# A residual added on TensorE: layer 0 of a two-layer model, the sum copied out by ScalarE

## The chip, the core and the metric

The kernel runs on one core of a Trainium2 chip. Five engines work side by side, each with its own queue of instructions in a fixed order: TensorE (PE in the profile, its weight loads as PEld), VectorE (DVE), ScalarE (ACT), GpSimd (POOL) and SyncE (SP), which here only starts transfers. TensorE reads SBUF and writes its sums to PSUM, in banks of 128 partitions x 512 float32; DVE and ACT can read and write PSUM and SBUF. The metric is the device time of one execution in microseconds, as the median of the runs shown; a profiled execution of its own gives the trace.

## What is computed

A batch of 2 sequences of 1024 rows, 512 wide, goes through two layers. Cut to what matters here:

```python
x = L0_attn_x                                   # (2, 1024, 512)
xn = layernorm(x)
x = x + L0_attn(xn) + L0_ffn(xn)                # layer 0
xn = layernorm(x)
x = x + L1_attn(xn) + L1_ffn(xn)                # layer 1

def L0_attn(x):                                 # one head of 128
    qkv = x @ Wqkv + bqkv
    q, k, v = split(qkv)
    out = softmax(q @ k.T / sqrt(128)) @ v
    return out @ Wo + bo                        # (1024, 128) @ (128, 512)

def L0_ffn(x):                                  # four streams of 128
    H_res = sinkhorn(logits(x), 50 rounds)      # 4 x 4 for each row
    ...
    return mix(H_res, x) + branch(x)
```

The change touches the first sum of layer 0: `x + (out @ Wo + bo)`.

## The kernel before

**Tiles.** A sequence is a batch `b` (0 or 1) of eight tiles `t` of 128 rows. `acc[b, t]` (128 x 512 float32, in SBUF for the whole kernel) is loaded with x (`load_x`, L124 to L127) and collects every term that is added to the residual stream. Matmuls take float16 operands: a float32 value is split into a high and a low half, and a product of two such values is three passes (`PASSES`, L81: high x high, high x low, low x high), all into one PSUM bank.

**Layer 0.** `front0(b)` makes the layer norm, transposes it into `xT` (through SP's DMA transposes, L242), and forms the logits of the Sinkhorn step (L385) and Q, K and V. `sinkhorn(b)` then runs 49 rounds; for batch 0 `chain_dve` does them on DVE, six small instructions a round (L576 to L578 and L581 to L583), each needing the one before, and at the end L592 and L527 write `Hm`, the 4 x 4 mixing matrix of each row. `attn0_rows` makes the score rows of four tiles at a time (L287 on DVE takes the row minimum out of PSUM, L291 on ACT the exponential, L305 to L314 the split on ACT, POOL and DVE, L320 the transposes on SP); `attn0_out` multiplies them with V and projects. `branch0` and `branch0_add` (POOL, L451 and L455) add the branch's output to `acc`. `mix0_units` mixes the streams by `Hm`: some tiles on ACT and POOL (L633, L634), some on DVE (L642), these after a copy of `acc` to PSUM by ACT (L614).

**`attn0_out`, which the change edits** (L467 to L488). Once for each half of a batch, four times in all. L476 and L478 on ACT and L479 on POOL turn the attention's output into two float16 halves `hl`. Then for each of four tiles a bank `p` is taken (`PP`, three banks in rotation, `BP` = 3). L484 puts the bias row `bo` into it, as two matmuls of one partition; L486 adds the three passes of the projection with `Wo`. All operands carry factors whose product is 1024. L488 on DVE scales the bank by 1/1024, adds `acc[b, t]` and writes the sum back to `acc[b, t]`.

**What sets the order.** The program is written as one long sequence of Python calls; a planner then orders the instructions of each engine by their place in the program and by a timeline that it simulates, and the queues are fixed before the run. So an instruction can stand in its queue ahead of its place in the text when the planner found it ready early: the bias rows L484 run long before the projection that they belong to. Steps of the Sinkhorn chain of batch 0 are drawn between the rows of attention by calls of `adv`. Buffers with one tag rotate through a fixed number of slots; the tag `tw` has one slot, which `ffn_block` of layer 1 uses from L954 on. POOL writes masks and constants at the very start (L111 to L120), then issues the loads of `Wlat` (L656).

**Layer 1.** `start` projects latents, Q, K and V from `xT` of batch 0's new layer norm, and `layer1_attn` runs eight groups of heads over both batches, with the rest of batch 1's layer 0 work (its Sinkhorn chain on POOL, its mix) and the feed-forward blocks laid between the rows.

Of the kernel before, what the change touches and what calls it, by code (L numbers as in the profile page):

```python
# [11 lines left out]
AF = mybir.ActivationFunctionType  # L12
ALU = mybir.AluOpType
# [3 lines left out]
P = 128  # L17
# [34 lines left out]
def tile_model(ctx: ExitStack, tc: tile.TileContext, out: bass.AP, a: dict):  # L52


    nc = tc.nc
    V, A, G = nc.vector, nc.scalar, nc.gpsimd
# [7 lines left out]
    def T(tag, shape, dt=F32, bufs=None):  # L64
        count[0] += 1
        kw = {} if bufs is None else {"bufs": bufs}
        return sb.tile(shape, dt, tag=tag, name=f"{tag}_{count[0]}", **kw)

    def C(name, shape, dt=F32):
        return const.tile(shape, dt, tag=name, name=name)  # L70

    def PP(shape=(P, 512)):
        count[0] += 1
        return ps.tile(list(shape), F32, tag="pp", name=f"pp_{count[0]}", bufs=BP)
# [40 lines left out]
        G.affine_select(mh, mh, [[-1, QR]], ALU.is_ge, NEG, base=0, channel_multiplier=1)  # L115
    ones = C("ones", [P, P], F16)
    G.memset(ones, 1.0)
    pm = C("pm", [P, 8])
    for e in range(8):
        G.memset(pm[:, e:e + 1], 8.0 - e)  # L120

    acc = {}
# [214 lines left out]
    def out_tile():  # L337
        count[0] += 1
        return ps.tile([P, 512], F32, tag="av", name=f"av_{count[0]}", bufs=BV)

    def attn_out(p, Vh, PT, nj):

        for j in range(nj):
            for k, (l, r) in enumerate(PASSES):
                nc.tensor.matmul(p, Vh(j, l), PT(r * nj + j),  # L345
                                 start=(j == 0 and k == 0),
                                 stop=(j == nj - 1 and k == 2))
# [120 lines left out]
    def attn0_out(b, half, Vh, PTs):  # L468

        p = out_tile()  # L470
        for k in range(2):
            attn_out(p[:, 256 * k:256 * k + 256], lambda j, l: Vh[:, j, l, :],
                     lambda n: PTs[k][:, n].rearrange("p a b -> p (a b)"), NT)
        ao = T("f2k", [P, 512], bufs=FB)
        bv = bqkv[:, 2:3]
        A.activation(ao, p, AF.Identity, bias=bv, scale=1.0 / PSCALE)  # L476
        hl = T("wo", [P, 2, 512], F16, bufs=WB)
        A.activation(hl[:, 0], ao, AF.Copy)  # L478
        G.tensor_tensor(hl[:, 1], ao, hl[:, 0], ALU.subtract)  # L479
        for q in range(4):  # L480
            t = 4 * half + q
            p = PP()
            for r in range(2):
                nc.tensor.matmul(p, row, bo[:, r], start=(r == 0), stop=False)  # L484
            for k, (l, r) in enumerate(PASSES):
                nc.tensor.matmul(p, hl[:, l, q * P:(q + 1) * P], wo0[:, r, :],  # L486
                                 start=False, stop=(k == 2))
            V.scalar_tensor_tensor(acc[b, t], p, 1.0 / 1024.0, acc[b, t], ALU.mult, ALU.add)  # L488

    def sinkhorn(b, lg):  # L490

# [487 lines left out]
    PTs = attn0_rows(0, 0, *f0[0][:2], lambda: adv(CA))  # L979
    ys0 = branch0(0, *f0[0][3:5], lambda: adv(CB))  # L980
    attn0_out(0, 0, f0[0][2], PTs)
    PTs = attn0_rows(0, 1, *f0[0][:2], lambda: adv(CA))
    attn0_out(0, 1, f0[0][2], PTs)
    for t in range(NT):
        branch0_add(0, t, ys0[t], f0[0][4])
# [3 lines left out]
    for half in range(2):  # L989
        if half:  # L990
            kv0[1][0]()
            kv0[1][1]()
        for hh in (2 * half, 2 * half + 1):
            load_q(0, hh)
        PTs = attn0_rows(1, half, *f0[1][:2], lambda: adv(CD))
        attn0_out(1, half, f0[1][2], PTs)
# [152 lines left out]
```

## Time and profile before

| what | value |
|---|---|
| runs shown | 1856.75, 1857.15, 1862.86 us (median 1857.15) |
| the profiled execution's own time | 1855.46 us |
| its span, from the first to the last instruction | 1853.7 us |
| busy over the span: PE / DVE / ACT / POOL | 1715.7 (93%) / 1447.6 (78%) / 1194.1 (64%) / 910.6 us (49%) |
| mean granted TensorE clock | 0.976 |
| L488 on DVE | 16 instructions, 0.680 us median, from 90.9 to 195.7 us |
| L486, L484 on PE | 48 and 32 matmuls |
| first matmul of layer 1 | 225.18 us |

The profile's page gives shares over the whole span. Layer 0 is the first eighth of it, and in the page's 40 slices (46 us each) PE's busy tenths read 4756 there, against 9 in almost every later slice, while DVE's read 8888. A view by stretches of time gives the busy time of each engine in each stretch; the timeline shows the instructions in order, with the idle time of the engine ahead of one in brackets and what ended it.

### The profile page before, as it was taken

To read this page: it belongs to the slowest core of one execution; us is meant where nothing else is said; L and a number is where in the kernel's file an instruction comes from. 1 tells how busy PE (TensorE), PEld (TensorE's weight loads), DVE (VectorE), ACT (ScalarE), POOL (GpSimd) and SP (SyncE) were. 2 spreads that over 40 slices of the span, in tenths; PEclk is the share of its full clock that TensorE was granted. 3 is DMA by queue.
4 is the path that set the end of the run, shared out by engine and by line. 5 is a ranking of instruction groups with operands and counts; after the bars stand their busy time and mean duration, and the time that the engine had idled before them with its cause. 6 is when DMAs were issued, how large, how long until landed. Compare 5 with 4: busy or idle time off the path is not lost. (4 is left out here: it accounts for less than half of the span.)

```text
span 1853.7 us, 35094 instructions
## 1 busy us (share of the span) xinstructions
PE 1715.7 (93%) x11458; PEld 1046.0 (56%) x11458; DVE 1447.6 (78%) x4050; ACT 1194.1 (64%) x2917; POOL 910.6 (49%) x1540
## 2 busy tenths in 40 slices
PE   4756399999999999998999999999999999999998
PEld 3434146566666556655555556666666666656565
DVE  8888978988888877777976867777777777777675
ACT  3848665656676778776544756666666767676554
POOL 5567639768775455647634333424242433335200
PEclk9878699999999999999999999999999999999999
DMA  7435225666574657468546555656565656566455
GB/s 211 82 56 124 67 51 131 143 115 144 113 147 102 143 115 158 111 131 158 137 92 141 130 120 126 146 111 150 107 151 115 142 117 140 117 141 139 101 123 120
DMA packets 707306, 230.26 MB, mean 124 GB/s; under 512 B 689953, under 2 KB 690081, under 8 KB 707122
## 3 DMA queue, kind: packets, MB, share of 16 engines
q1 hardware_dynamic: 691666, 180.75, 47.2%
q0 software_dynamic: 13152, 43.07, 8.5%
q10 hardware_dynamic: 2304, 4.20, 0.7%
q8 instruction: 90, 1.47, 0.4%
q14 instruction: 94, 0.77, 0.1%
HBM read 52.81 MB, written 4.19 MB: 31 GB/s over the span
## 5 line engine op out<-in xcount | busy, mean ns | idle before, releaser
L291 ACT ACTIVATE P<-P,nm 128x1024 f32<-128x1024 f32 (+31 forms) x528 | 391.3, 742 | 250.0 <-DVE nm L283 234.8
L314 DVE SCALAR_TENSOR_TENSOR Phl<-P,r,Phl 128x1024 f16<-128x1024 f32 (+31 forms) x515 | 434.4, 853 | 85.9 <-ACT Phl L308 79.5
L88 PE MATMUL s<-K,Q 128*128 128x512 f16 (+22 forms) x2400 | 440.7, 317 | 19.5 <-DVE P L287 11.6
L345 PE MATMUL av<-PT,V 128*128 128x256 f16 x3648 | 447.7, 274 | 7.5 <-DMA PT<-Phl 6.8
L345 PEld LDWEIGHTS <-V 128*128 128x128 f16 x3648 | 357.0, 98 | 94.7 <-DMA PT<-Phl 8.3
L308 ACT ACTIVATE Phl<-P,r 128x1024 f16<-128x1024 f32 (+31 forms) x515 | 370.0, 731 | 22.3 <-DMA PT<-Phl 3.3
L88 PE MATMUL pp<-xT,wq 128*128 128x512 f16 x1536 | 372.9, 381 | 6.3 <-DVE acc L737 3.2
L88 PE MATMUL pp<-wo,ao 128*128 128x512 f16 x1536 | 369.9, 379 | 2.9 <-ACT ao L104 2.7
L94 POOL TENSOR_SCALAR f2k<-f2k 128x512 f32<-128x512 f32 x164 | 109.5, 668 | 499.9 <-DVE Phl L314 444.5
L88 PEld LDWEIGHTS <-Q 128*128 128x128 f16 x2400 | 223.2, 98 | 178.2 <-issue 28.4
L88 PEld LDWEIGHTS <-wq 128*128 128x128 f16 x1536 | 149.6, 98 | 173.8 <-issue 8.5
L88 PEld LDWEIGHTS <-ao 128*128 128x128 f16 x1536 | 149.4, 98 | 156.5 <-ACT ao L104 4.8
L287 DVE TENSOR_SCALAR_CACHE_REDUCE P<-s 128x512 f32<-128x512 f32 (+15 forms) x272 | 152.6, 562 | 21.7 <-PE s L88 19.7
L283 DVE CUSTOM_DVE_ANT_0 P<-s,mask,nm 128x272 f32<-128x272 f32 (+15 forms) x256 | 157.3, 615 | 8.7 <-PE s L88 1.0
L303 ACT ACTIVATE r<-r 128x1 f32<-128x1 f32 x528 | 96.2, 193 | 66.2 <-DVE r L302 65.4
L319 POOL MEMSET Phl<- 128x192 f16 (+2 forms) x384 | 72.6, 209 | 133.5 <-DMA PT<-Phl 95.7
L302 DVE RECIPROCAL r<-r 128x1 f32<-128x1 f32 x528 | 79.2, 155 | 75.3 <-ACT P L291 72.1
L104 ACT ACTIVATE ao<-av 128x512 f16<-128x512 f32 x128 | 75.1, 587 | 92.2 <-PE av L345 92.0
L283 DVE CUSTOM_DVE_ANT_0 P<-s,mask 128x32 f32<-128x32 f32 (+15 forms) x256 | 104.3, 432 | 27.6 <-PE s L88 27.1
L104 ACT ACTIVATE Q<-pp 128x512 f16<-128x512 f32 x128 | 74.5, 582 | 76.7 <-PE pp L88 72.2
L737 DVE SCALAR_TENSOR_TENSOR acc<-pp,acc 128x512 f32<-128x512 f32 x128 | 87.4, 682 | 41.0 <-PE pp L88 40.6
L105 DVE SCALAR_TENSOR_TENSOR Q<-pp,Q 128x512 f16<-128x512 f32 x128 | 87.6, 684 | 34.9 <-ACT Q L104 34.6
(254 smaller groups left out, 2119.1 us busy)
## 6 DMA issues: line engine op xcount, KB each, us to landing
f2k<-in_Wq POOLq DMA_DIRECT2D x64, 256.0 KB, 3.2
f2k<-in_WoT POOLq DMA_DIRECT2D x64, 256.0 KB, 3.3
PT<-Phl SPq DMA_TRANSPOSE x528, 3.2
acc<-in_x SPq DMA_DIRECT2D x16, 256.0 KB, 4.6
f2k<-in_Wup POOLq DMA_DIRECT2D x16, 256.0 KB, 3.5
out<-acc ACTq DMA_DIRECT2D x16, 256.0 KB, 3.5
xr<-in_x SPq DMA_DIRECT2D x12, 256.0 KB, 4.1
f2k<-in_Wlat POOLq DMA_DIRECT2D x8, 256.0 KB, 5.5
```

Source lines behind the costliest of these rows:

```text
L88: nc.tensor.matmul(dst, lhs(l), rhs(r), start=(i == 0 and j == 0), stop=(i == n - 1 and j == 2))
L94: first = G.tensor_scalar(stage, stage, scale, 1.0, ALU.mult, ALU.mult)
L104: A.activation(hl_hi, src, AF.Copy, scale=scale)
L105: return V.scalar_tensor_tensor(hl_lo, src, scale, hl_hi, ALU.mult, ALU.subtract)
L283: last_row[0] = V.tensor_tensor_reduce(Pm[:, o:o + w], pt[:, :w], mask[:, 512 - w:], -scale, first, ALU.add, ALU.min, nm[:, k:k + 1])
L287: last_row[0] = V.tensor_scalar(Pm[:, o:o + w], pt[:, :w], -scale, first, ALU.mult, ALU.min, accum_out=nm[:, k:k + 1])
L291: A.activation(Pm[:, :W], Pm[:, :W], AF.Exp, bias=last, scale=-1.0, accum_out=r[:, 0:1])
L303: A.activation(r[:, 1:2], r[:, 1:2], AF.Copy, scale=PSCALE)
L308: A.activation(hl[:, 0, :W], Pm[:, :W], AF.Copy, scale=r[:, 1:2])
L314: lo = V.scalar_tensor_tensor(hl[:, 1, :W], Pm[:, :W], r[:, 1:2], hl[:, 0, :W], ALU.mult, ALU.subtract)
L345: nc.tensor.matmul(p, Vh(j, l), PT(r * nj + j), start=(j == 0 and k == 0), stop=(j == nj - 1 and k == 2))
L737: V.scalar_tensor_tensor(acc[b, t], p, 1.0 / 256.0, acc[b, t], ALU.mult, ALU.add)
```

## The change

In layer 0 the addition of the residual moves from DVE into the PSUM bank. A 128 x 128 float32 matrix `eye` with 1024 on its diagonal is made by POOL at the start, in the slot of tag `tw`. In `attn0_out` one more matmul, a float32 product of `eye` and `acc[b, t]`, goes into the bank between the two bias rows and the three passes. The bank then holds 1024 times the whole sum, and an ACT copy with scale 1/1024 takes the place of L488.

```diff
     ones = C("ones", [P, P], F16)
     G.memset(ones, 1.0)
+    eye = T("tw", [P, P], bufs=1)
+    G.memset(eye, 1024.0)
+    G.affine_select(eye, eye, [[-1, P]], ALU.is_equal, 0.0, base=0, channel_multiplier=1)
     pm = C("pm", [P, 8])
...
             for r in range(2):
                 nc.tensor.matmul(p, row, bo[:, r], start=(r == 0), stop=False)
+
+            nc.tensor.matmul(p, eye, acc[b, t], start=False, stop=False)
             for k, (l, r) in enumerate(PASSES):
                 nc.tensor.matmul(p, hl[:, l, q * P:(q + 1) * P], wo0[:, r, :],
                                  start=False, stop=(k == 2))
-            V.scalar_tensor_tensor(acc[b, t], p, 1.0 / 1024.0, acc[b, t], ALU.mult, ALU.add)
+            A.activation(acc[b, t], p, AF.Copy, scale=1.0 / 1024.0)
```

## The prediction

> **What bounds the kernel now.** I read the cut into stretches of time first, because the shares over the whole span mix two different kernels: layer 0, up to about 225 us, and layer 1. Columns: stretch and length in us, then busy us (and instructions) of PE, PEld, DVE, ACT, POOL, then granted clock, DMA share, GB/s.
>
> ```profile
> 40.00:118.00 78.00, 49.98 (x309) 27.07 (x306) 69.70 (x232) 49.60 (x103) 46.56 (x44) 0.81 0.34 73
> 118.00:131.00 13.00, 9.75 (x101) 8.29 (x102) 8.50 (x36) 6.58 (x18) 6.45 (x6) 0.82 0.85 142
> 131.00:174.00 43.00, 34.19 (x243) 19.54 (x241) 38.82 (x138) 35.53 (x77) 28.46 (x33) 0.92 0.30 70
> 174.00:197.00 23.00, 15.00 (x83) 7.70 (x82) 19.56 (x56) 10.58 (x17) 15.06 (x16) 0.93 0.61 157
> 197.00:225.00 28.00, 0.00 (x0) 0.00 (x0) 27.15 (x91) 22.70 (x72) 20.69 (x18) 0.51 0.21 40
> 1072.00:1853.00 781.00, 775.45 (x5157) 479.18 (x5156) 568.56 (x1550) 496.80 (x1189) 255.24 (x473) 1.00 0.59 127
> ```
>
> The last row is layer 1, where PE is busy 775 of 781 us; the change puts nothing there. In layer 0 the fullest engine is DVE: 69.70 + 8.50 + 38.82 + 19.56 = 136.6 of the 157 us from 40 to 197. PE works 108.9 of them at a granted clock of 0.81 to 0.93, and nothing at all from 197 to 225. So what ends layer 0 is looked for on DVE, in the order of time:
>
> ```profile
> 185.53 1.29 DVE L488 SCALAR_TENSOR_TENSOR acc<-pp,acc 128x512 f32<-128x512 f32 x2 [0.96 <-PE pp L486]
> ...
> 193.46 0.69 DVE L488 SCALAR_TENSOR_TENSOR acc<-pp,acc 128x512 f32<-128x512 f32 x1 [0.71 <-PE pp L486]
> ...
> 195.72 0.63 DVE L488 SCALAR_TENSOR_TENSOR acc<-pp,acc 128x512 f32<-128x512 f32 x1
> 196.26 0.28 DVE L592 TENSOR_TENSOR sk<-sk,sk 128x128 f32<-128x128 f32 x1
> 196.57 0.33 DVE L527 TENSOR_SCALAR Hm<-sk,gs 128x128 f32<-128x128 f32 x1
> ...
> 197.00 9.45 ACT L633 ACTIVATE f2k<-xr,Hm 128x128 f32<-128x128 f32 x32 [0.82 <-DVE Hm L527]
> ...
> 198.35 3.71 POOL L634 TENSOR_TENSOR acc<-acc,f2k 128x512 f32<-128x512 f32 x3 [5.44 <-ACT f2k L633]
> ...
> 225.18 9.57 PE L88 MATMUL pp<-xT,PT 128*128 128x512 f16 x36 [29.63 <-DMA xT<-wo]
> ```
>
> The Sinkhorn chain of batch 0 (L576 to L583, six small DVE instructions in about 1.03 us per half round) ends in L592 and L527, which writes Hm. ACT and POOL wait for Hm, mix the streams, the layer norm and transposes follow, and PE, idle for 29.63 us, takes up layer 1 at 225.18. What comes before L592 on DVE therefore delays everything, and that includes all sixteen L488, which stand between the steps of the chain.
>
> **The change part by part.** *Removed from DVE.*
>
> ```profile
> L488 DVE SCALAR_TENSOR_TENSOR acc<-pp,acc x16: 627/680/693, 90.9 to 195.7; 128x512 f32<-128x512 f32 x16
> ...
>   PE pp L486: 3.0, 4
> ```
>
> From the start of one to the start of the next DVE instruction an L488 takes about 0.61 us (90.86 to 91.47), since neighbours overlap a little: 16 x 0.61 = 9.8 us. DVE also stood 3.0 us in front of four of them, waiting for PE: 0.50 and 0.85 in the first eight, 0.96 and 0.71 in the last eight. The last eight fall where only the chain is left on DVE (174 to 197), so their 8 x 0.61 + 1.67 = 6.5 us come off directly. The first eight (90.9 to 106) are worth 4.9 + 1.35 = 6.2 us, but may be lost again at the next place where DVE waits:
>
> ```profile
> DVE lg L385 <- PE pp L88: 4.2, 2, 2.7
> ```
>
> L385 of batch 1 (120.4 us) waits for xT of batch 1, which comes through POOL, ACT and the transposes, not through DVE. If the order on DVE stays, DVE comes there early and waits longer. If the planner, which orders by its own timeline, fills the hole with further chain steps, the gain is kept; between 152 and 158.6 us it has done so, with six half rounds of L576 to L583 in front of an L287 that had to wait for POOL. Bounds for this half: 0 and 6.2; I take 5.0, nearer to kept.
>
> *Added on ACT.* Sixteen copies with a constant scale, PSUM to SBUF. The nearest rows copy the same shape between the same memories the other way, or write f16:
>
> ```profile
> L614 ACT ACTIVATE s<-acc x2: 576/576/577, 171.4 to 173.0; 128x512 f32<-128x512 f32 x2
> ```
>
> With 0.59 each this is 9.4 us on ACT. ACT idles where they come: 11.4 us before L476 at 99.36, 10.2 us before L233 at 110.86, 4.35 us before L611 at 188.83, 3.3 us before L614 at 194.98. Cost: nothing, as long as the copy does not wait in front of work that is needed. Behind it in ACT's queue would stand L614 and, above all, L633, on which POOL's L634 and the mix wait. POOL's L455 (batch 0) and bank reuse by L484 now wait for the copy instead of L488, 0.59 against 0.68 us: no loss. If that cover is gone, the copies cost at most their 9.4 us.
>
> The Trainium skill has a rule against this part ("ScalarE: Activation LUTs", section on rules for kernel authors): adds and multiplies belong on VectorE. The rows here have DVE at 0.68 us for the fused add and ACT at 0.58 for a copy of the same shape, and DVE is the fuller engine; by the rule the copies would stay on DVE and the sum would be nil, by the rows it is the one below.
>
> *Added on PE.* Sixteen float32 products 128x128 by 128x512. No float32 matmul is in this trace, so its price is bounded. From below: one f16 pass of that size, 0.216 us (24 in 5.18 us at full clock). From above: each operand as two f16 halves gives four products, at the slow clock of the stretch at 67 us:
>
> ```profile
> 66.99 2.72 PE L88 MATMUL s<-K,Q 128*128 128x512 f16 x6 [2.88 <-DVE P L287]
> ...
> 92.27 0.82 PE L486 MATMUL pp<-wo,wo 128*128 128x512 f16 x3
> ...
> 94.86 4.46 PE L345 MATMUL av<-PT,V 128*128 128x256 f16 x24 [0.81 <-DMA PT<-Phl]
> ...
> 190.17 1.46 PE L484 MATMUL pp<-wo,row 1*128 1x512 f16 x6
> ```
>
> 2.72 / 6 x 4 = 1.8 us. I take 1.0: the three f16 passes of L486 take 0.82 with their tail, a fourth adds 0.216. The skill has a price ("FP8 and Floating Point Precision", TensorE precision notes): true float32 is four passes through the array; as an estimate from that, four times 0.216 is 0.87 us, and the total 14 us instead of 16. No run here has shown it.
>
> So 16 us of PE work is added (3.5 to 29). The product needs only acc and the bank, so it can run with the two bias rows (L484), which PE does long before the rest: three banks per half. Of the four in each half, three fall into PE's holes: after 64.1 (2.88 idle), at 93 to 95 and 99.3 (0.81 and 0.9), after 155.8 (4.7), at 191 (0.6). The fourth waits for a bank, and costs its full 1.0. Late next: batch 0's first half by 3.0 - 2.9 = 0.1; its second half by 2 x 1.0 - 0.8 in front of av and 1.0 - 0.9 behind it, 1.3, and with them xT of batch 1; then batch 1's attention, whose last L488 ended at 196.3, by the fourth product of its first half, 1.0, and by 4 x 1.0 - 0.6 = 3.4 in its second. That is 5.8 in all, so it ends near 202. Nothing on the way to Hm waits for that end; the first 1.4 us can show at L385, where chain steps may fill, and I charge 1.5.
>
> *The unit matrix* on POOL at the start: a 128x128 memset and one affine select; rows near them are 0.20 and 0.20 us for smaller tiles, say 0.5 to 1.0 in all. POOL then waits 3.57 us for its Wlat loads, whose issue is late by as much, and 1.71 us at 18.09 for ACT; that covers it, and without it 1 us is lost. Its tile is used again only in layer 1. No SP or DMA work is moved.
>
> Sum: 6.5 + 5.0 - 1.5 = 10.0 us earlier Hm; 197 to 225 is a chain through DVE, ACT and POOL that moves along, and layer 1 behind it is filled by PE. The profiled execution's 1855.5 becomes 1845.5; it lies 1.7 below the median 1857.15, so the forecast is **1847 us**. Bounds of the forecast's own case: 6.2 + 6.5 without charge gives 1844.5, 6.5 - 1.5 = 5 gives 1852; with 3 us for layer 1's order on either side, 1841 to 1854.
>
> **Rivals.** *The end of batch 1's attention takes the place of Hm.* If the planner puts its last L476, L478, L479 and copies before L633 and L634 in the queues of ACT and POOL, an earlier Hm is worthless. For: before, they did stand there, L479 at 191.76 and L614 at 194.98. Against: they stood there because they were ready 5 us before Hm; with Hm at 187 the order should turn. POOL's L479 alone in front puts L634 at 195 for 198.35: 1854. The copies in front too, the last ending 0.6 after 202.1: L633 starts 5.7 late, 1863. Middle 1858.
>
> *Slower: PE.* The place is the same queue, the price that of the float32 product. At 1.8 us each, the four halves are late by 5.4 - 2.9, 5.4 - 1.7, 5.4 - 4.7 + 1.8 and 7.2 - 0.6, or 15.3 us: attention ends at 211.6, the last copy 0.6 later, and L633 starts 15.2 late: 1872. It decides, with the bound of 0.5% below, from about 1.3 us a product, where the same sum gives 9, and only if the copies stand before L633. For: PE's clock in layer 0 is 0.81, and idle stretches lower it to 0.5. Against: three in four run in holes.
>
> **How the numbers follow.** Forecast 0.55, attention's end 0.22, PE 0.23. What a measurement can tell here is about 0.5%, 9.3 us, so faster means under 1847.9 and slower over 1866.4. Of the forecast's 0.55, 0.44 lies below 1847.9 and 0.11 within; of the second, 0.17 within and 0.05 above (layer 1's order moving against it too); of the third 0.20 above and 0.03 within. That makes 0.44, 0.31, 0.25. The range takes in the forecast's own 1841 to 1854, the second case, and the lower edge of the third: 1841 to 1867.
>
> **What would show it.** Right: no L488 on DVE, L527 near 187 instead of 196.57, PE's first layer-1 matmul near 215 instead of 225.18, PE's share from there unchanged. L385's wait grown to 8 us means the first half was lost. The float32 product's own row gives its price. L633 waiting for a copy or for PE, with Hm long ready, is the first rival; PE late by more than 10 us at 190 the second. Wrong altogether: layer 1 takes longer than its 1628 us from 225.18 to the end by more than 3 us.

## The result, and the profile after

The changed kernel takes 1869.33 us in the median of five runs (1866.71 to 1874.12), the kernel before 1857.15 us beside it (1856.75 to 1862.86). The ratio is 1.0063, with a 95% interval from 1.0042 to 1.0084: slower by 0.6%, where faster by 0.5% was forecast, and above the range. The profiled execution took 1871.66 us, span 1869.9 us.

The view by stretches of the changed kernel, in the stretches that the prediction showed (length, then busy us of PE, PEld, DVE, ACT, POOL, then granted clock, DMA share, GB/s):

```profile
40.00:118.00 78.00, 55.96 (x330) 29.42 (x328) 69.99 (x225) 53.34 (x109) 48.27 (x45) 0.86 0.31 70
174.00:197.00 23.00, 16.03 (x58) 6.83 (x56) 19.03 (x63) 14.16 (x21) 16.87 (x16) 0.70 0.69 171
197.00:225.00 28.00, 14.15 (x49) 5.46 (x48) 15.29 (x52) 20.39 (x61) 15.96 (x13) 0.66 0.00 1
1072.00:1853.00 781.00, 780.30 (x5205) 481.89 (x5203) 578.07 (x1573) 507.84 (x1210) 260.36 (x481) 1.00 0.60 128
```

In the last row layer 1 is as full as before. The difference is in the third row: PE, which had nothing to do from 197 to 225 us, now still works there on layer 0's attention, and DVE, which was busy for 27 us of this stretch, is busy for 15. So the stretch that mixes the streams has moved to a later time. The timeline of PE in the changed kernel shows what is late (start, length, engine, line, operation, in brackets the idle time before it and what ended it):

```profile
181.99 0.82 PE L491 MATMUL pp<-wo,wo 128*128 128x512 f16 x3 [0.18 <-POOL wo L482]
185.89 1.01 PE L487 MATMUL pp<-wo,row 1*128 1x512 f16 x2 [3.08 <-ACT acc L493]
186.83 2.08 PE L489 MATMUL pp<-acc,tw 128*128 128x512 f32 x2
188.69 1.49 PE L491 MATMUL pp<-wo,wo 128*128 128x512 f16 x3
190.12 1.03 PE L487 MATMUL pp<-wo,row 1*128 1x512 f16 x2
191.07 2.08 PE L489 MATMUL pp<-acc,tw 128*128 128x512 f32 x2
192.94 4.09 PE L348 MATMUL av<-PT,V 128*128 128x256 f16 x24
...
200.05 2.78 PE L348 MATMUL av<-PT,V 128*128 128x256 f16 x24
...
234.09 10.82 PE L88 MATMUL pp<-xT,PT 128*128 128x512 f16 x36 [16.96 <-DMA xT<-wo]
```

and the timeline of ACT in the same stretch, then the row on DVE that writes Hm, then the end of batch 1's attention in the kernel before, PE's last `av` and ACT's scaling of it:

```profile
184.21 1.15 ACT L311 ACTIVATE Phl<-P,r 128x1024 f16<-128x1024 f32 x1 [2.17 <-DMA PT<-Phl]
185.26 1.55 ACT L493 ACTIVATE acc<-pp 128x512 f32<-128x512 f32 x3
...
202.93 0.69 ACT L479 ACTIVATE f2k<-av,bqkv 128x512 f32<-128x512 f32 x1 [7.15 <-PE av L348]
203.52 3.60 ACT L638 ACTIVATE f2k<-xr,Hm 128x128 f32<-128x128 f32 x12
```

```profile
193.26 0.33 DVE L532 TENSOR_SCALAR Hm<-sk,gs 128x128 f32<-128x128 f32 x1
```

```profile
187.46 2.78 PE L345 MATMUL av<-PT,V 128*128 128x256 f16 x24
190.34 0.69 ACT L476 ACTIVATE f2k<-av,bqkv 128x512 f32<-128x512 f32 x1
```

(Lines after the diff's first part are three higher than before, lines after `attn0_out` five, and in the other kernels a few more or less: L476 is L479, L484 is L487, L486 is L491, L527 is L532, L633 is L638; L489 is the float32 product, L493 the copy.) Hm is written at 193.3 us, 3.3 us earlier than before. But the mix on ACT, L638, starts at 203.5 us, 6.5 us later than before: L479, the last scaling of batch 1's attention, stands ahead of it in ACT's queue and waits 7.15 us for PE. PE in turn waited 3.08 us for a bank which an ACT copy was to free, and that copy stood on ACT behind L311, which waited for a transfer. In the kernel before, PE's wait for a bank at this place (L484 for L488, at 186.28 us) was 0.35 us. The first matmul of layer 1 comes at 234.09 instead of 225.18.

### The profile page after: what moved, and what is told of

It reads as the page before. It is cut to its first block, busy times and chain, and to the rows that moved or that the text cites. A ratio compares the mean times of both kernels' runs of the same rounds, so it can differ in the third digit from the quotient of the medians.

```text
span 1869.9 us, 35155 instructions
## 1 busy us (share of the span) xinstructions
PE 1746.4 (93%) x11490; PEld 1055.0 (56%) x11490; DVE 1442.7 (77%) x4034; ACT 1201.2 (64%) x2933; POOL 914.5 (49%) x1542
## 5 line engine op out<-in xcount | busy, mean ns | idle before, releaser
L311 ACT ACTIVATE Phl<-P,r 128x1024 f16<-128x1024 f32 (+31 forms) x515 | 369.8, 731 | 22.3 <-DMA PT<-Phl 6.5
L104 ACT ACTIVATE ao<-av 128x512 f16<-128x512 f32 x128 | 75.1, 587 | 92.1 <-PE av L348 91.8
L104 ACT ACTIVATE Q<-pp 128x512 f16<-128x512 f32 x128 | 74.5, 582 | 75.9 <-PE pp L88 71.5
```

Of the source, the lines that this page charges most:

```text
L104: A.activation(hl_hi, src, AF.Copy, scale=scale)
L311: A.activation(hl[:, 0, :W], Pm[:, :W], AF.Copy, scale=r[:, 1:2])
```

## The experiments

Five moments are read from each trace (us): the last attention scaling on ACT (before: L476), Hm on DVE, the start of the mix on ACT, the first matmul of layer 1, and the first sum that layer 1 adds to `acc` on DVE (before: L737; it lies behind both norms and the start of layer 1). The ratio is that of each run's own comparison, with its interval.

| run | attention | Hm | mix | layer 1 | first sum | ratio |
|---|---|---|---|---|---|---|
| before | 190.3 | 196.6 | 197.0 | 225.2 | 287.7 | |
| before, second profile | 190.3 | 196.6 | 197.0 | 225.4 | 288.2 | |
| the change | 202.9 | 193.3 | 203.5 | 234.1 | 298.1 | 1.0063 (1.0042 to 1.0084) |
| the change again | 200.9 | 194.0 | 201.4 | 232.2 | 294.7 | 1.0062 (1.0045 to 1.0080) |
| e1: product, copy on DVE | 192.4 | 193.9 | 195.2 | 225.1 | 290.2 | 1.0019 (1.0005 to 1.0033) |
| e2: copy on ACT, no product | 189.9 | 190.1 | 190.5 | 221.7 | 288.4 | 1.0000 (0.9988 to 1.0012) |
| e3: batch 0 alone | 195.7 | 194.5 | 196.3 | 225.9 | 290.9 | 1.0029 (1.0016 to 1.0043) |
| e4: batch 1 alone | 200.4 | 200.2 | 201.0 | 232.3 | 295.2 | 1.0033 (1.0021 to 1.0044) |
| e4b: all but batch 1's last half | 196.7 | 193.2 | 197.3 | 226.8 | 296.5 | 1.0043 (1.0027 to 1.0059) |
| g1: batch 0's first half alone | 188.9 | 191.6 | 192.1 | 221.9 | 285.5 | 1.0005 (0.9988 to 1.0023) |
| e5: change, last half held | 202.7 | 191.2 | 192.7 | 223.3 | 291.6 | 1.0027 (1.0013 to 1.0041) |
| e6: before, last half held | 204.1 | 194.4 | 194.8 | 226.8 | 294.8 | 1.0037 (1.0023 to 1.0051) |
| e7: product behind the passes | 203.4 | 196.6 | 204.0 | 235.3 | 303.3 | 1.0083 (1.0062 to 1.0104) |
| e9: norm steps ahead on ACT | 205.3 | 195.7 | 205.9 | 236.5 | 303.2 | 1.0074 (1.0056 to 1.0091) |
| e8: both, and evictions behind | 207.1 | 199.5 | 207.7 | 238.2 | 306.8 | 1.0098 (1.0074 to 1.0122) |
| e12: twelve tiles, product behind | 205.8 | 198.4 | 206.4 | 235.9 | 298.4 | 1.0052 (1.0034 to 1.0071) |
| f1: e7, copies ahead | 197.9 | 190.9 | 198.4 | 229.5 | 296.9 | 1.0077 (1.0054 to 1.0101) |
| f2: batch 1's first half on DVE | 199.1 | 196.0 | 199.7 | 230.9 | 300.9 | 1.0075 (1.0052 to 1.0098) |
| f5: batch 1's last half on DVE | 199.5 | 193.0 | 200.0 | 229.6 | 296.1 | 1.0069 (1.0047 to 1.0092) |
| f3: batch 1's copies on DVE | 200.2 | 197.2 | 200.8 | 230.2 | 295.0 | 1.0047 (1.0033 to 1.0061) |

The column of the first sum is the one that goes with the time. Over the 18 profiles below those of before (the change is there twice), the time lost by the ratio is on average 1.0 us more than the lateness of the first sum against the first profile of before (standard deviation 2.1 us, largest gap 5.1 us, correlation 0.92). So most of what the change costs is there by 300 us, in layer 0 and in the passage to layer 1.

### One part alone

The product kept, and the copy done by DVE:

```diff
-            A.activation(acc[b, t], p, AF.Copy, scale=1.0 / 1024.0)
+            V.tensor_scalar(acc[b, t], p, 1.0 / 1024.0, None, ALU.mult)
```

> The float32 product stays, the copy goes back to DVE (a scaling of the bank, no add). Theory A (the copy on ACT: banks wait for ACT's queue, and the copies and L479 stand before the mix there): without ACT copies the attention of batch 1 ends on time, DVE has its sixteen instructions back, so about the time before, 1857 to 1861. Theory B (the product: PE is late whatever engine empties the bank): the loss stays, 1866 to 1872, and the last product of layer 0 on PE ends after 210 us in its trace.

The copy on ACT, and no product, so that layer 0's first sum lacks x:

```diff
-            nc.tensor.matmul(p, eye, acc[b, t], start=False, stop=False)
```

> The ACT copy stays, the float32 product is left out, so the residual x is missing from layer 0's first sum. Theory A: the loss stays, 1865 to 1871, with L487 waiting for ACT copies by some 3 us and L638 behind L479. Theory B: PE is on time, DVE is relieved, the mix starts near 190 instead of 197, 1846 to 1852.

The product alone costs 0.19%, the copy on ACT alone nothing (0.00%), the two together 0.63%. So neither price explains the loss: theory A comes close in the first run and fails in the second, theory B fails in both, and what has to be found is where the two parts meet. e2 also shows that an earlier Hm is not yet a gain: Hm and mix are 6.5 us earlier than before, the first matmul 3.5, and the first sum 0.8 us later. In that run the norm of the first four tiles is ready for ACT at 204.3 us and gets its first step there at 208.0, behind the mix of the second four tiles; before it came 0.4 us after it was ready.

### Which tiles

The change for batch 0 alone, for batch 1 alone, for all but the last half of batch 1, and for the first half of batch 0 alone; the other tiles keep the addition on DVE. The edit, for batch 0:

```diff
-            nc.tensor.matmul(p, eye, acc[b, t], start=False, stop=False)
+            if b == 0:
+                nc.tensor.matmul(p, eye, acc[b, t], start=False, stop=False)
...
-            A.activation(acc[b, t], p, AF.Copy, scale=1.0 / 1024.0)
+            if b == 0:
+                A.activation(acc[b, t], p, AF.Copy, scale=1.0 / 1024.0)
+            else:
+                V.scalar_tensor_tensor(acc[b, t], p, 1.0 / 1024.0, acc[b, t], ALU.mult, ALU.add)
```

For the others the condition reads `b == 1`, `(b, half) != (1, 1)` and `(b, half) == (0, 0)`.

> The change for batch 0 alone; batch 1 adds on DVE as before. If the loss comes from batch 1's last halves: L633's place as before, Hm 0 to 4 us earlier, 1853 to 1859. If it comes from batch 0 (the products in front of av, xT of batch 1 late, the chain's logarithm step in ACT's way): 1863 to 1870.

> Product and ACT copy for batch 1's eight tiles alone; batch 0's stay as before. Theory C (the loss is a convoy at the end of batch 1's attention: the product stands on PE ahead of the average of the values, the banks come free from ACT's queue, and the last scaling of that attention stands on ACT ahead of the mix): most of the change's loss comes with batch 1: first layer-1 matmul at 229 to 234 us (before 225.2, the whole change 234.1), last attention scaling at 198 to 203, time +0.35 to +0.7% (1864 to 1871). Theory D (every copy put on ACT costs its share, wherever it stands): half of the loss, +0.3% (1863), and the first layer-1 matmul near 227.

> Product and ACT copy for twelve tiles, all but the last half of batch 1. Theory C: without products and copies in the last half the last scaling of the attention comes at 194 to 198 us and the first layer-1 matmul at 225 to 228; time +0.1 to +0.35% (1859 to 1864). Theory D: three quarters of the loss stay, +0.45 to +0.5% (1866 to 1867).

> The change for the first half of batch 0 alone: four products, four copies on ACT. If the loss comes from ACT's queue beside batch 1's norm (the second half's copies at 101 to 104 us), this half costs nothing: first row's maximum of batch 1 at 140 to 143 us, time -0.1 to +0.1%. If each quarter costs its share (theory D), 143.5 to 145 and +0.13 to +0.2%.

Batch 0 costs 0.29%, batch 1 0.33%, and 0.62% together: by batch the losses add up, as theory D has it, though the attention's end and the first matmul of e4 (200.4 and 232.3) are those of theory C. But the losses hardly go by the tile. Batch 0's first half costs nothing that can be told (1.0005, and the interval does not shut out D's 0.13%), and its trace is early, not late: batch 1's first row at 139.3 us where D had 143.5 to 145, the first sum 2.2 us ahead of before. So batch 0's loss most likely comes with its second half, though the intervals of e3 and g1 still overlap. And e4b, for which theory C named the attention's end (194 to 198; 196.7) and the first matmul (225 to 228; 226.8) rightly, still lost 0.43%, more than C allowed and next to D's three quarters. Both theories are too simple: C lays too much of the loss on batch 1's last half, and D has g1's trace late where it is early.

What batch 0's second half does is seen beside g1, PE first in the changed kernel, then in g1:

```profile
91.78 0.60 PE L487 MATMUL pp<-wo,row 1*128 1x512 f16 x2
92.31 1.13 PE L489 MATMUL pp<-acc,tw 128*128 128x512 f32 x2
93.37 0.60 PE L487 MATMUL pp<-wo,row 1*128 1x512 f16 x2
93.90 1.13 PE L489 MATMUL pp<-acc,tw 128*128 128x512 f32 x2
94.86 2.78 PE L348 MATMUL av<-PT,V 128*128 128x256 f16 x24
```

```profile
91.80 0.81 PE L487 MATMUL pp<-wo,row 1*128 1x512 f16 x3
92.54 2.79 PE L348 MATMUL av<-PT,V 128*128 128x256 f16 x24
```

Two rows with their products stand ahead of `av`, which starts 2.3 us later, and with it the scaling (97.69 against 95.37 us), the branch's additions on POOL and the norm of batch 1 (L236 at 109.18 against 106.87). These 2.3 us show against g1 alone: in the two profiles of before the scaling came at 99.36 and 96.84 us and the norm at 110.86 and 108.33, so here the change is still no more than 0.9 us late. Then 2.7 us more are lost on ACT, where the Sinkhorn chain's logarithm has come to stand among the norm's instructions (the changed kernel):

```profile
115.12 0.80 ACT L236 ACTIVATE f2k<-acc,rsa 128x512 f32<-128x512 f32 x1
118.71 0.23 ACT L591 ACTIVATE sk<-sk 128x32 f32<-128x32 f32 x1 [2.79 <-DVE sk L588]
118.84 0.61 ACT L241 ACTIVATE wo<-f2k 128x512 f16<-128x512 f32 x1
```

ACT waits 2.79 us for DVE, with the norm's L241 behind. On DVE, L588 stood behind a step of 3.71 us, and the chain then waits for ACT in turn:

```profile
114.70 3.71 DVE L592 TENSOR_TENSOR sk<-sk,sk 128x128 f32<-128x128 f32 x1 [1.04 <-ACT sk L590]
118.97 0.29 DVE L593 TENSOR_TENSOR sk<-sk,sk 128x128 f32<-128x128 f32 x1 [0.29 <-ACT sk L591]
121.78 0.29 DVE L582 TENSOR_REDUCE sk<-s 128x32 f32<-128x128 f32 x1 [2.37 <-ACT s L574]
```

In g1 the same two logarithms come at 117.36 and 118.18 us without a wait. This pair, ACT's wait of 2.8 us and DVE's step of 3.7, stands in both profiles of the change and in e3, e4b, e5, e7, e8, e9, e12, f2, f3 and f5, and in no run that leaves batch 0's second half as it was (before, e4, e6, g1) or has its copies on DVE (e1); e2, without the product, has a step of 3.20 us and no such wait. It is the clearest trace of batch 0's part. It is not needed for a loss, though: in f1 the wait is 0.56 us and the step 1.48, and the loss 0.77%. Batch 1's first row of attention reaches DVE at 144.26 us in the change and at 139.26 in g1. The two profiles of before have 142.72 and 140.48 there, though, and agree again from Hm on, so 2.2 us of that difference are no more than the spread between two profiles of one kernel.

### The last half of batch 1 held behind the mix

The last call of `attn0_out` comes after the mix of the first four tiles, once in the changed kernel and once in the kernel before:

```diff
-        attn0_out(1, half, f0[1][2], PTs)
+        if half == 0:
+            attn0_out(1, 0, f0[1][2], PTs)
...
+        if k == 0:
+            attn0_out(1, 1, f0[1][2], PTs)
```

> The whole change, but the last attn0_out (batch 1, second half) is called after the mix of the first four tiles, so that the planner puts L638 ahead of L479 and of the last four copies in ACT's queue, and nothing else before that place moves. If the queue place of L479 is the loss: L638 starts within 1.5 us of Hm (194 to 195), the first matmul of layer 1 lies at 222 to 226 instead of 234, and the time is 1856 to 1862. If the loss lies elsewhere (late xT, the order in layer 1): 1866 to 1872 again.

> The kernel before, with the last half of batch 1's attention output called after the mix of the first four tiles, as in the run that held it in the changed kernel. Theory C: the hold itself is worth little where nothing stands in front of the mix: mix start 195 to 197.5 us, time within 0.15% of before (1855 to 1860), and then the +0.27% of the held change is what the change still costs. Rival: the hold itself costs 0.2 to 0.3% (it delays the second four tiles), 1861 to 1863; then the change costs nothing beside it.

In the changed kernel the mix now follows Hm (191.2) at 192.7 us, and over half of the loss is gone (1.0027 against 1.0063). That is what the reading of the profile above asks for: L479 ahead of the mix is a part of the cause. But the hold is no free repair: the kernel before loses 0.37% by it, as the rival said. Its mix starts 2.2 us earlier, and its first sum comes 7.2 us later, because the second four tiles need the held half, and the norm's steps for them are mixed with layer 1's first evictions. Held, the two kernels' ratios differ by 0.1%, less than either interval: with the hold in both, no loss of the change is left to see. Since the hold itself costs as much, this does not say which part of the loss the queue place of L479 makes.

### A second profile of each kernel

> The changed kernel once more, for a second profile beside the runs above. If the further loss at the crossover of layer 1's two batches (5 us in the first profile) belongs to the change, it comes again, and the time is +0.6%; if it is a spread between runs, the second profile shows another figure there, while the first layer-1 matmul stays within 1.5 us of 234.1.

> The kernel before once more, for a second profile: first row's maximum of batch 1 within 1 us of 142.7, Hm within 1 us of 196.6, first layer-1 matmul within 1 us of 225.2. If it is further off than 2 us, single traces do not bear the readings above.

The change again: 1868.31 us against 1856.24, ratio 1.0062; first matmul at 232.2. From the first layer-1 matmul to the end of the span the two profiles of the change take 1635.8 and 1631.5 us, the two of before 1628.5 and 1631.4. So of the 7.3 us which the first pair of profiles showed in layer 1 the second pair has 0.1; two profiles of one kernel differ by 2.9 us there for before and by 4.3 for the change, and nothing shows that layer 1 is slower by the change. The kernel before again took 1858.59 us in its one execution. Hm and the first matmul came within 0.2 us of the first profile, but batch 1's first row 2.2 us earlier, beyond the 2 us set in its expectation: a reading of that row from a single trace is good to 2 us at best.

### The product behind the passes, and ACT's order

In e7 each product comes last in its bank:

```diff
-            nc.tensor.matmul(p, eye, acc[b, t], start=False, stop=False)
...
-                                 start=False, stop=(k == 2))
+                                 start=False, stop=False)
+            nc.tensor.matmul(p, eye, acc[b, t], start=False, stop=True)
```

> The whole change, with one thing moved: the float32 product of each tile comes behind the three passes of the projection, as the last of its bank, so that it can't stand on PE ahead of the average of the values. ACT's copies stay. Theory C2 (the loss needs the product ahead of the average: it waits there for a bank that ACT must empty, and the end of attention goes with it): last attention scaling at 190 to 196 us (201 to 203 in the two profiles of the change), first layer-1 matmul at 224 to 229 (232 to 234), time +0.1 to +0.4% (1858 to 1864). Theory D (each copy and product costs its share wherever it stands, as the halves of the change by batch suggest: +0.29 and +0.33 make +0.62%): last scaling at 199 or later or not, the time stays +0.5 to +0.65% (1866 to 1868).

In e9 the product stays in front, and two copies of `mix0_units` are queued on ACT behind the exponential of the first four tiles' norm:

```diff
-                    A.activation(got["d"], acc[b, t], AF.Copy)
+                    with after(*([last_exp[0]] if t >= 4 else [])):
+                        A.activation(got["d"], acc[b, t], AF.Copy)
```

> The whole change; only the two copies of the second four tiles into their banks ahead of the second mix are held on ACT behind the two small steps (logarithm, exponential) of the first four tiles' norm. In the change these steps come 4.0 us after their input is ready (221.0 against 217.0), before it 0.4. Theory E (place in ACT's queue is a part of its own): these steps at 217.5 to 219.5, first layer-1 matmul at 229.5 to 232, time +0.4 to +0.55% (1864 to 1866). Theory C2 alone: what ACT gains for the first four tiles the second four lose, layer 1's query product starts at 246 to 249 as in the change, time +0.6%.

(`last_exp` is the last exponential that the norm's `rsqrt` put on ACT.) e8 has both, and layer 1's first evictions behind the norm of the second four tiles:

```diff
         for mc in range(4):
-            lat_evac(0, mc, 0, lat_block(0, wl[:, mc], 0))
+            p = lat_block(0, wl[:, mc], 0)
+            with after(last_rs[1], last_exp[0]):
+                lat_evac(0, mc, 0, p)
```

> Both: the product behind the passes, the first norm's steps on ACT ahead of the second four tiles' copies, and layer 1's first evictions on ACT and DVE behind the norm of the second four tiles. C2 and E together: last attention scaling 190 to 196 us, first layer-1 matmul 222 to 227, query product of layer 1 at 237 to 242, time -0.1 to +0.25% (1854 to 1861). If D holds, +0.5% or more in spite of it.

e12 is e4b with the product behind the passes, by the diffs above:

> The change for twelve tiles (batch 0, and the first half of batch 1), with the product behind the passes; the last four tiles as before, added on DVE. ACT has no added copy in the stretch in which it makes the mix. C2 and E: Hm done at 190 to 194 us, last attention scaling 189 to 193, first layer-1 matmul at 220.5 to 224.5, query product at 236 to 241, time -0.15 to +0.2% (1853.5 to 1860). D: three quarters of +0.62%, so +0.45% (1864.5), as the twelve tiles with the product in front measured (+0.43%).

All four were misses. Their ratios lie above those of the change, or for e12 above that of e4b, but only e8's by more than the noise of both. Taking the product out of `av`'s way does not bring the attention's end forward. ACT in e7 shows what took its place:

```profile
182.53 1.15 ACT L311 ACTIVATE Phl<-P,r 128x1024 f16<-128x1024 f32 x1 [2.31 <-DMA PT<-Phl]
195.22 1.52 ACT L616 ACTIVATE P<-P,rsa 128x512 f32<-128x512 f32 x2 [11.55 <-DMA P<-in_x]
196.65 0.57 ACT L493 ACTIVATE acc<-pp 128x512 f32<-128x512 f32 x1
...
203.40 0.69 ACT L479 ACTIVATE f2k<-av,bqkv 128x512 f32<-128x512 f32 x1 [1.39 <-PE av L348]
```

The planner has put L616, a scaling of x for the second four tiles, ahead of the copies of batch 1's first half. It waits 11.55 us for its load; the copies wait behind it, a bank stays taken, and PE's next row and the rest of `av` come late again. In e9 ACT's small norm steps still come 2.9 us after their input (219.4, 222.3), now behind the last L493 copy. So C2 and E fall as sufficient repairs: changing one order gives the planner another.

### The copies that free the banks

f1 is e7 with L616 for the second four tiles queued behind the copies of batch 1's first half (`last_copy[1, 0]` is the last of them):

```diff
-                A.activation(xr, xr, AF.Identity, scale=rs[:, 2, t:t + 1], bias=rs[:, 1, t:t + 1])
+                with after(*([last_copy[1, 0]] if t >= 4 else [])):
+                    A.activation(xr, xr, AF.Identity, scale=rs[:, 2, t:t + 1], bias=rs[:, 1, t:t + 1])
```

> The product behind the passes as in the run before, and on ACT the scaling of x for the second four tiles held behind the four copies of batch 1's first half. Theory F (PE waits for a bank that ACT's queue frees late, and the average of the values behind it goes along): the copies come at 190 to 194 us instead of 196.7 to 201.4, last attention scaling at 197 to 200.5 (203.4), first layer-1 matmul at 229 to 233 (235.3), time +0.5 to +0.7% (+0.83). If the release does not matter, 203 and +0.8% again.

f2, f5 and f3 are the change with the copies of batch 1's first half, last half or both on DVE, the products kept:

```diff
-            A.activation(acc[b, t], p, AF.Copy, scale=1.0 / 1024.0)
+            if (b, half) == (1, 0):
+                V.tensor_scalar(acc[b, t], p, 1.0 / 1024.0, None, ALU.mult)
+            else:
+                A.activation(acc[b, t], p, AF.Copy, scale=1.0 / 1024.0)
```

with `(1, 1)` in f5 and `b == 1` in f3.

> The whole change, but the copies of batch 1's first half (four of the sixteen) on DVE, the product kept. F: PE's wait for the bank (3.1 us at 185.9) goes; last attention scaling at 194 to 199.5, first layer-1 matmul at 226 to 230.5, time +0.25 to +0.45%. Rival G (only the number of copies among the mix counts): last scaling 201 to 203, first matmul 232 to 234, time +0.6%.

> The whole change, but the copies of batch 1's last half on DVE, the product kept. F: last attention scaling stays at 201 to 203.5, mix start with it; the four copies are missing among the mix (2.4 us), first layer-1 matmul 229.5 to 232.5; time +0.45 to +0.6%. G: first matmul 227 to 229, time +0.2 to +0.4%.

> The whole change, but all eight copies of batch 1 on DVE, the product kept; batch 0's stay on ACT. F and G: last attention scaling 194 to 199, first layer-1 matmul 224.5 to 228.5, time +0.15 to +0.35% (between the run with the product alone, +0.19, and that with batch 0 alone, +0.29). If the product alone makes the end late once ACT is loaded by batch 0's copies, last scaling 200 or later and +0.5%.

For the attention's end F holds where it moves the release of banks: 197.9 us in f1 instead of 203.4 in e7, 199.1 in f2 instead of 200.9 and 202.9. For the time it fails: f1 1.0077, f2 1.0075, no better than the change. f5 fits neither F nor G. f3 has no copy of batch 1 on ACT, and its attention still ends at 200.2 us with a loss of 0.47%: that is the last case of its expectation, the products late by themselves once ACT is loaded by batch 0's copies; no run isolates this.

Why 3 us won at the first matmul are lost again is seen in f2 at the norm of the second four tiles, ACT and then DVE:

```profile
234.23 0.20 ACT L204 ACTIVATE rs<-ve 128x4 f32<-128x4 f32 x1 [6.24 <-DVE ve L224]
235.51 0.38 ACT L104 ACTIVATE cmp<-pp 64x256 f16<-64x256 f32 x1 [1.08 <-PE pp L88]
235.79 0.19 ACT L205 ACTIVATE rsb<-rs 128x4 f32<-128x4 f32 x1
```

```profile
235.92 0.42 DVE L105 SCALAR_TENSOR_TENSOR cmp<-pp,cmp 64x256 f16<-64x256 f32 x1 [1.73 <-ACT cmp L104]
...
239.20 0.53 DVE L227 SCALAR_TENSOR_TENSOR rsb<-mvb,rsb 128x4 f32<-128x4 f32 x1
```

The norm's exponential L205 stands on ACT behind an eviction L104 that waits for PE; its DVE steps stand between further evictions. From L224, which makes the variance, to the end of L227 f2 takes 6.1 us (233.66 to 239.73), the kernel before 2.5 (228.04 to 230.56) and 3.2 in its two profiles, the change 3.3 and 2.5. Other runs with an early first matmul show the same: e4b 5.8, e5 5.2, e2 5.2, f5 5.2, f1 4.2 us; so do e6 with 6.2, and e7 with 7.0 and e9 with 4.5, whose first matmul was late. This second gate is one reason why the first matmul alone does not tell the time.

No run beat the kernel before: e2 equals it, but leaves x out, and g1, whose profile had the first matmul 3.3 us earlier, equals it too.

## Why the prediction was wrong

**The costs of the parts held.** The product was priced at 1.0 us. These are its own rows in the changed kernel, two records for each product, then the rows of the copy, with who waited for it:

```profile
L489 PE MATMUL pp<-acc,tw x32: 592/697/1222, 58.8 to 214.8; 128*128 128x512 f32 x32
```

```profile
L493 ACT ACTIVATE acc<-pp x16: 575/594/603, 88.7 to 220.5; 128x512 f32<-128x512 f32 x16
...
  PE pp L487: 4.5, 3
```

From its start to the next instruction's a product takes 0.96 us (93.90 to 94.86), but 1.87 (191.07 to 192.94) where PE's granted clock is low. The Trainium skill ("FP8 and Floating Point Precision", TensorE precision notes) counts four passes for true float32, from which the prediction estimated 0.87 us; the row at the high clock is about a tenth above that. The copy was priced at 0.59 and is 0.594. POOL's unit matrix took 0.5 us, and the first product, at 58.75 us, did not wait for it.

The second rival, a product of 1.3 us or more, does not hold by its price at the high clock. But its sign, PE late by more than 10 us at 190, was met: the last `av` before the scaling starts at 200.05 us instead of 187.46. The product alone does not do this, since in e1 the attention's end is 2.1 us late; with the copies on ACT the bank comes late, and the products behind that wait run at half the granted clock.

**"Nothing on the way to Hm waits for that end"** is the step that failed, together with the sentence behind it in the first rival, "with Hm at 187 the order should turn". Hm does not wait for the end of batch 1's attention, but the mix does, by ACT's queue, and the order did not turn: L479 stayed ahead of L638. The planner's order does not follow what is ready in the run: L479 could start only 9.3 us after Hm was written (202.93 against 193.59), and it still stood first. That is the first rival's mechanism. A second step failed with it, the one that made the attention's end so late: "bank reuse by L484 now wait for the copy instead of L488, 0.59 against 0.68 us: no loss" counted how long the copy runs and not what it stands behind on ACT. PE waited 3.08 us for it where it had waited 0.35.

The first rival had 0.22 and a price of 1858, or 1863 with the copies in front; it came to more for three reasons that can be read off, all against the first profile of before:

- The end was sized at 202 us for the last copy, 5.8 us late. The scaling L479 alone is 12.6 us late: 1.5 at batch 1's first row, 3.7 more by the eighth row's exponential, and 7.3 from there to L479, with PE's 3.1 us wait for a bank and four products ahead of the end that take 5.8 us. Two of these take 1.87 us each, from 186 to 194 us, where the granted clock was 0.50 (1.00 before); the other two take 1.06 and 0.96. In the second profile of the change one of the four takes 1.87, and the end is 2.1 us earlier. Against the second profile of before the three parts are 3.8, 3.7 and 5.1, so the split between the first and the last is firm to about 2 us only. Before there were 6.7 us of room between the attention's end (190.34) and the mix (197.00), so about 6 us show: the mix is 6.5 us late. The rival had 5.7.
- "197 to 225 is a chain that moves along" did not hold: from mix to first matmul 30.6 us instead of 28.2, with the last half's copies (0.59 each), L481 and the two L619, which before stood ahead of the mix, now among it on ACT. The norm's first step there, L204, comes 4.0 us after its input is made (217.02 to 221.00), where before it came after 0.4 (210.67 to 211.03). The copies were to cost "nothing, as long as the copy does not wait in front of work that is needed"; here they stood in front of it.
- From the first matmul to layer 1's first sum 64.0 us instead of 62.5.

6.5 + 2.4 + 1.5 is 10.4 us, the lateness of the first sum; the medians differ by 12.2, and the last 1.8 are within the spread of the first sums against the ratios.

**Hm 10 us earlier** became 3.3. The 16 x 0.61 us left DVE as counted, but the charge for batch 1's lateness (1.5) was too small. DVE waited for ACT instead: at 114 to 122 us the chain's logarithm goes through ACT, whose queue is then full of batch 1's norm, and DVE's chain stands 1.0, 0.3 and 2.4 us for it, with one step of 3.71 us (the rows stand under "Which tiles"). L388's wait for PE, named as the sign of a lost first half, was 3.2 us, not 8: it was lost elsewhere. Where Hm did come at 190.1 (e2), the gain was used up in ACT's queue before layer 1.

**Layer 1 unchanged** held as far as two profiles of each kernel can tell: 1631.4 and 1631.5 us by the second ones, 1628.5 and 1635.8 by the first. The sign set for "wrong altogether", over 3 us, was met by the first profiles and is too fine for one trace of each. In the sum of the bounds, 1852 with 3 us on top is 1855 and not 1854; nothing hangs on it.

**What stays open.** Shown are the sum above, that neither part alone loses it, and that the loss by batch adds up. Not shown is a single link whose removal gives the time back: every order tried for it (e5, e7, e8, e9, e12, f1 and the copies on DVE in f2, f3, f5) left or made another wait. The part of the eight rows' order on ACT (3.7 us) was not tried by itself.

## What to carry to other kernels

Before moving work onto an engine that is idle on average, list what stands behind it in that engine's queue, and what the freed buffer or bank lets go: here a 0.59 us copy held a PSUM bank, the bank held PE's next row, and PE held the instruction ahead of the mix on the same ACT. An "off the path" end has a measured room (6.7 us here); sum the lateness of every part of the change against it before calling it free. And where a planner sets the order, one repaired wait gives another order, so compare a moment behind all of these waits, as the first sum of layer 1 here, and not the first matmul.

## What the runs showed of the hardware that was not expected

A float32 product of 128x128 by 128x512 appears as two matmul records and two weight loads. It costs 0.96 us at the high clock and 1.87, nearly twice that, at 187 and 191 us: there, from 186 to 194 us, the granted clock was 0.50, against 1.00 in the kernel before, where PE's wait for a bank was 0.35 us. In the second profile of the change it was 0.70 over the same 8 us, and only the product at 187 took 1.87 us. So the wait for the bank was followed by products at twice their price, just ahead of the attention's end.

One 128x128 step of the chain took 3.71 us on DVE (L592, from 114.70), where such steps take 0.29 us; POOL worked on its elementwise instructions without a pause from 114.78 to 118.27. In g1 two such steps took 1.53 and 1.06 us, and in the kernel before 0.33 and 1.06, POOL busy too. No run tried whether the one causes the other.
